# Two attentions of a decoder: issuing scores, maxima and values by whole steps of two key chunks

## The chip, the cores and the metric

The kernel runs on one core of a Trainium2 chip. The metric is device time in microseconds (us) of one launch; lower is better. Three runs of the kernel before gave 3532.81, 3535.61 and 3540.02 us, median 3535.61.

Five engines work side by side, each through its own queue of instructions: TensorE (PE; its weight loads are shown apart as PEld), VectorE (DVE), ScalarE (ACT), GpSimd (POOL) and SyncE (SP, which here only issues DMAs). They are held in order by semaphores. Matrix products land in PSUM, which has 8 banks of 128 partitions x 512 fp32 numbers.

## The reference

Four decoder layers follow one another on x (8 batches x 256 tokens x 128). Each layer adds a cross-attention over a context of 1601 tokens x 64 per batch, and then a feed-forward block. Attentions 0 and 3 are alike: 16 heads of width 8. With q, k and v projected from the layer norm of x and from the context, cut to what matters:

```python
scores = jnp.einsum('bhqd,bhkd->bhqk', qh, kh) * scale      # 256 x 1601 for each of 16 heads
attn = jax.nn.softmax(scores, axis=-1)
out = jnp.einsum('bhqk,bhkd->bhqd', attn, vh)
x = x + out.transpose(0, 2, 1, 3).reshape(B, LQ, D_MODEL) @ Wo + bo
```

Attentions 1 and 2 and the feed-forward blocks are other functions of the kernel, which the change does not touch.

## The kernel before

`narrow` computes attentions 0 and 3. Its work is cut into 32 **units**: 8 batches, and in each four groups of four heads (n = 4b + i). A unit goes through the keys in 13 chunks of 128 (the last has 65), two chunks to a **step**, so 7 steps p = 0 to 6; the last step has one chunk. The four heads of a unit lie in two tiles of K and Q, t = 0 and 1, with two heads each (g = 0 and 1), in rows 0 to 63 and 64 to 127. Each step is cut into two **half steps**, one for each t.

Three kinds of work run through each other on PE:

- **Scores**, `score(p, t, e)`, L1069: for two chunks and two heads, four matmuls of K (64 rows x 128 keys as weights) with Q (256 queries) into two banks `st`. ACT takes the exponential of each bank (L1072) into the tile `e`, which holds all four heads of one step and has two buffers. The maximum of each row is already subtracted: the shift lies in extra rows of Q.
- **Values**, `values(c, e)`, L1081: for one chunk, the four heads' `e` times V, each head in its own 32 columns of the array, summed over the 13 chunks in the one bank `ov`. Each of these fp32 products is shown as two matmuls, so a chunk is 8. The values of a step are issued in the step after it, from the list `before`. When the last chunk is done, ACT copies the bank (L1085) and SP sends it off by two DMAs (L1087, L1088).
- **Maxima**, `maxima(n)`, L873 and L876: before a unit starts, the largest score of each of its rows is needed. For this all scores are computed a first time with queries as weights: 14 pieces for a unit, each a `pair` of matmuls in two banks `pm` (g = 0 and 1; 64 rows x 128 queries, 512 keys wide). DVE reduces each bank with a TENSOR_REDUCE. Pieces 7 and 14 are narrow (66 keys, both halves of the queries in one bank, four matmuls). Then `shift` (three small DVE instructions) and, later, `place_shift` (a transpose on PE, L895, a copy on ACT and two DMAs) put the result into Q.

PSUM is divided by `psum(m=3, s=4, o=1)`: three banks `m` for the maxima, four banks `s` for the scores and for all side work (`bank()`), one `o` for the values. The banks of each kind are handed out in turn, and an instruction that writes a bank waits until the last reader of the bank's former use is done.

The order of instructions is written by hand (`manual_schedule`): the order in which the functions call is the order in each engine's queue. `plan(m)` gives the 14 pieces of the maxima of unit m to slots, one slot for each half step: from slot DONE of unit m - 2 to slot DONE of unit m - 1, with the shift in the last of them. DONE is 8 of 14. So in most half steps there is one piece, of the unit after the next or of the next. In the first unit, all 14 pieces of unit 1 stand in its first DONE slots.

`beside` is a list of side work with the share of the unit at which each piece is due: placing K and Q of unit n + 3 by DMA (L846 on SP; L855 and L856 on POOL), `place_shift`, and, by the head group i of the unit, the next batch's turned input and queries (i = 0: L808, L814), its K (i = 0: L777), its V (i = 1: L834), the end of the batch before (i = 2: two reciprocals on DVE, L907, and the projection, L913), and the turned context of the batch after the next (i = 2, attention 0: L761; attention 3 loads it ready). From unit 26 on (AFTER), pieces of the next block's first batch join it.

A half step issues, in this order: the four scores of its t; one chunk of values of the step before, if one is left; the side work that is due; the maxima of its slot.

Of the kernel before, what the change touches and what calls it, by code (L numbers as in the profile page):

```python
# [49 lines left out]
TAKEN = -3.0e38  # L50
KW = LK + 1
RING = 4
DONE = 8
AFTER = 26


# [1 line left out]
def decoder_kernel(ctx: ExitStack, tc: tile.TileContext, a: dict, out: bass.AP):  # L58
# [36 lines left out]
    def load_later(n):  # L95
        for out, in_ in later[:n]:
            nc.sync.dma_start(out=out, in_=in_)
        del later[:n]
# [248 lines left out]
    def run(steps, names):  # L347
        for name in names:
            for step in steps:
                if name in step:  # L350
                    step[name]()
# [322 lines left out]
    def narrow(wq, wkT, wvT, wo, bq, bk, bv, bo, first, after=None, last=None):  # L674
# [8 lines left out]
        with ExitStack() as es:  # L683
# [174 lines left out]
            def place(n, t):  # L858
                place_keys(n, t)
                place_queries(n, t)  # L860

            def maxima(n):

                mx = two.tile([P, QT, 4, 4], F32, tag="mx", name="mx", bufs=3)
                last = KW - 1536

                def pair(t, js, at, w):
                    k, q = K[n % RING][t], Q[n % RING][t]
                    pt = [pm() for g in range(2)]
                    for x, j in enumerate(js):  # L870
                        for g in range(2):
                            r = slice(64 * g, 64 * g + 64)
                            nc.tensor.matmul(pt[g][:, x * w:(x + 1) * w], lhsT=q[r, j * P:(j + 1) * P],  # L873
                                             rhs=k[r, at:at + w], start=True, stop=True)
                    for g in range(2):
                        nc.vector.tensor_reduce(mx[:, js[0]:js[-1] + 1, 2 * t + g, at // 512],  # L876
                                                pt[g][:, 0:len(js) * w].rearrange("p (j k) -> p j k", k=w),
                                                AX.X, ALU.max)

                def shift():  # L880
                    m = two.tile([P, QT, 4], F32, tag="mxn", name="mxn")
                    nc.vector.tensor_reduce(m, mx, AX.X, ALU.max, negate=True)
                    mq = M[n % 2].rearrange("p j (h s) -> p j h s", s=8)
                    nc.vector.tensor_copy(mq[:, :, :, 0], m)
                    nc.vector.tensor_tensor(mq[:, :, :, 1], m, mq[:, :, :, 0].bitcast(F32), ALU.subtract)

                order = [(j, at) for at in (0, 512, 1024) for j in range(QT)]
                return [f for t in range(2) for f in
                        (*(lambda j=j, t=t, at=at: pair(t, (j,), at, 512) for j, at in order),
                         lambda t=t: pair(t, range(QT), 1536, last))], shift  # L890
# [116 lines left out]
            before = []  # L1007
            steps = (NC + 1) // 2
            per = 2 * steps
            tasks = {}  # L1010

            def plan(m):

                pairs, shift = maxima(m)
                first_, last_ = max(0, per * (m - 2) + DONE), per * (m - 1) + DONE
                for x, f in enumerate(pairs):
                    tasks.setdefault(first_ + (last_ - first_) * x // len(pairs), []).append(f)
                tasks[last_ - 1].append(shift)

            plan(1)  # L1020
            for n in range(units):
                b, i = divmod(n, 4)
                v = V[b % 2]
                if n + 2 < units:
                    plan(n + 2)

                beside = []
                if n + 3 < units:
                    beside += [((0.0, 0.25)[t], lambda t=t: place(n + 3, t)) for t in range(2)]
                beside.append((0.3, lambda: load_later(3)))  # L1030
                if n + 1 < units:
                    beside.append(((DONE + 1) / per, lambda: place_shift(n + 1)))
                if b + 1 < NB and i == 0:
                    beside += zip((0.0, 0.2, 0.5, 0.65, 0.8, 1.0),
                                  (lambda: turn_y(b + 1), lambda: make_q(b + 1), *make_k(b + 1)))
                if b + 1 < NB and i == 1:
                    beside += zip((0.2, 0.4, 0.6, 0.8), make_v(b + 1))
                if b and i == 2:
                    beside += zip((0.2, 0.35, 0.6), finish(b - 1))
                if b + 2 < NB and i == 2:  # L1040
                    load_ct(b + 2)
                    if first:
                        cuts, turns = make_ct(b + 2)
                        beside += zip((0.0, 0.0, 0.4, 0.6), cuts)
                        beside += zip((0.3, 0.5, 0.7, 0.9), turns)
                if b + 3 < NB and i == 3:
                    beside.append((0.0, lambda: load_raw(b + 3)))
                if b + 2 < NB and i == 3:
                    beside.append((0.5, lambda: (make_y(b + 2), add_bias(b + 2))))
                if after is not None and n >= AFTER:  # L1050
                    if n == AFTER:
                        late = after(left(), bank)
                    beside += [((x - per * (n - AFTER)) / per, lambda x=x: run([late[x]], EARLY + LATE))
                               for x in late if x // per == n - AFTER]
                beside.sort(key=lambda x: x[0])
                if i == 0:
                    od[b] = two.tile([P, LQ], F32, tag="od", name="od")
                    sums[b] = two.tile([P, LQ], F32, tag="sums", name="sums")
                cell = {}

                def score(p, t, e):
                    k, q = K[n % RING][t], Q[n % RING][t]
                    cs = range(2 * p, min(2 * p + 2, NC))
                    m = P if cs[-1] < NC - 1 else LAST
                    st = [bank().rearrange("p (j q) -> p j q", q=LQ) for g in range(2)]
                    for j, c in enumerate(cs):
                        for g in range(2):
                            r = slice(64 * g, 64 * g + 64)
                            nc.tensor.matmul(st[g][0:m, j, :], lhsT=k[r, c * P:c * P + m], rhs=q[r, :],  # L1069
                                             start=True, stop=True)  # L1070
                    for g in range(2):
                        nc.scalar.activation(e[0:m, 2 * t + g, 0:len(cs), :], st[g][0:m, 0:len(cs), :], AF.Exp)  # L1072

                def values(c, e, cell=cell, i=i, v=v, b=b):
                    if c == 0:
                        cell["o"] = ps["o"].tile([P, LQ], F32, tag="o", name="ov")
                    m = P if c < NC - 1 else LAST
                    for g in range(4):
                        h = 4 * i + g
                        at = 2 * D * c + 32 * (h // 2) + 2 * (h % 2)  # L1080
                        nc.tensor.matmul(cell["o"][32 * g:32 * g + 32, :], lhsT=v[0:m, at:at + 32],  # L1081
                                         rhs=e[0:m, g, c % 2, :], start=(c == 0), stop=(c == NC - 1))
                    if c == NC - 1:
                        os = two.tile([P, LQ], F32, tag="os", name="os")
                        nc.scalar.copy(os, cell["o"])  # L1085
                        at = slice(32 * i, 32 * i + 32)
                        nc.sync.dma_start(out=od[b][at, :], in_=os[0:P:4, :])  # L1087
                        nc.sync.dma_start(out=sums[b][at, :], in_=os[1:P:4, :])  # L1088

                for p in range(steps):  # L1090
                    e = two.tile([P, 4, 2, LQ], F32, tag="e", name="e")
                    for t in range(2):
                        score(p, t, e)
                        if n == p == 0:
                            spare(6)
                        if before:
                            before.pop(0)()
                        while beside and (beside[0][0] * 2 * steps < 2 * p + t + 1 or p * t == steps - 1):
                            beside.pop(0)[1]()
                        for f in tasks.pop(per * n + 2 * p + t, []):  # L1100
                            f()
                    before = [lambda c=c, e=e, values=values: values(c, e)
                              for c in range(2 * p, min(2 * p + 2, NC))]
            *inverses, project = finish(NB - 1)
# [829 lines left out]
```

## Time and profile before

The table is of one profiled execution. Its span, from the first instruction to the last, is 3529.4 us; the median of the runs is 3535.61 us, 6.2 us more.

| stage | from - to, us | PE busy | DVE busy | ACT busy | POOL busy | PE clock |
|---|---|---|---|---|---|---|
| attention 0 (units) | 55.5 - 706 | 643.1 | 535.6 | 519.9 | 297.3 | 0.99 |
| the blocks between | 706 - 2686 | 1873.4 | 1354.3 | 1200.1 | 607.2 | 0.98 |
| attention 3 (units) | 2686 - 3317 | 625.5 | 536.6 | 500.9 | 212.4 | 1.00 |
| the last block | 3317 - 3529.4 | 202.3 | 121.2 | 57.3 | 21.6 | 1.00 |

| unit by head group, steady | attention 0, us | attention 3, us |
|---|---|---|
| i = 0 | 20.82 | 20.82 |
| i = 1 | 21.10 | 21.10 |
| i = 2 | 20.28 | 19.19 |
| i = 3 | 17.83 | 17.77 |

How to read it: a unit's length is the time from its first score to the next unit's first score. PE's busy time is a union of matmul times whose ends are modelled, so a PE that is busy all the time can still have stretches in which nothing new begins; the starts of matmuls and of weight loads (PEld) tell more. In a row of the timeline stand start, length, engine, line, operation, out<-in, count, and in brackets the idle time of that engine before the row with what ended it. In a row of a stage stand its stretch and length, then the busy time and the number of instructions of each engine, the PE clock, the DMA share and GB/s.

### The profile page before, as it was taken

The numbers are of one execution on the slowest core, as the hardware profiler recorded it, in microseconds if no ns is written. First come the engines' busy times: TensorE is split into PE (matmuls) and PEld (weight loads), VectorE is DVE, ScalarE is ACT, GpSimd is POOL, SyncE is SP. The second block draws the span as 40 slices with busy tenths as digits, with TensorE's granted clock in tenths as the row PEclk, the third lists the DMA queues.
The fourth block names the chain that finished last, engine by engine and source line by source line (L and its number), as shares of the span: only waits on it lengthen the run. The fifth ranks groups of instructions, "written<-read, shape, count | busy, mean of one in ns | idle before, by whom it ended". The sixth has DMA issues, their size and how long they took to land.

```text
span 3529.4 us, 75160 instructions
## 1 busy us (share of the span) xinstructions
PE 3380.6 (96%) x28453; PEld 2299.7 (65%) x28453; DVE 2580.6 (73%) x6482; ACT 2290.0 (65%) x5747; POOL 1179.4 (33%) x2105
## 2 busy tenths in 40 slices
PE   7999999989999999999999999988999999999999
PEld 4555555468787877788787878866445555555444
DVE  6888888656776767676776767675557888888665
ACT  3888887746666666667666666654224878787622
POOL 6344344624152513324151520131115333332100
PEclk8999999989999999999999999999998999999999
DMA  5544444120001001000100000021004444443100
GB/s 97 89 73 74 71 77 58 19 83 1 15 1 33 2 1 39 1 15 1 39 1 22 6 1 15 1 66 33 1 0 85 78 63 68 65 69 53 41 5 7
DMA packets 113449, 130.24 MB, mean 37 GB/s; under 512 B 67616, under 2 KB 96832, under 8 KB 112448
## 3 DMA queue, kind: packets, MB, share of 16 engines
q1 hardware_dynamic: 92352, 114.22, 18.0%
q0 software_dynamic: 20480, 10.53, 1.3%
q8 instruction: 225, 3.69, 0.4%
q10 hardware_dynamic: 256, 0.69, 0.1%
q14 instruction: 136, 1.11, 0.1%
HBM read 44.79 MB, written 11.28 MB: 16 GB/s over the span
## 4 chain that ended last, share of the span: by engine, by line
PE 81%; DVE 9%; ACT 6%; POOL 2%; issue 2%; DMA 0%; DVEq 0%; POOLq 0%; SPq 0%; ACTq 0%
PE ov L1081 13%; PE o L514 12%; PE st L467 12%; PE pm L873 11%; PE t L500 8%; PE st L1069 6%; PE gu L1740 3%; PE o L1789 3%; PE gu L1741 3%; ACT pt L502 3%; DVE ls L474 2%; DVE mx L876 2%; ACT e L488 2%; PE st L834 1%; DVE ql L444 1%
## 5 line engine op out<-in xcount | busy, mean ns | idle before, releaser
L876 DVE TENSOR_REDUCE mx<-pm 128x1 f32<-128x512 f32 (+1 forms) x1792 | 1020.3, 627 | 172.7 <-PE pm L873 168.9
L1072 ACT ACTIVATE e<-st 128x512 f32<-128x512 f32 (+1 forms) x1792 | 910.6, 566 | 210.5 <-PE st L1069 160.0
L474 DVE TENSOR_REDUCE ls<-st 128x1 f32<-128x512 f32 x1088 | 549.5, 567 | 292.3 <-PE st L467 291.2
L488 ACT ACTIVATE e<-st,ls 128x512 f32<-128x512 f32 x1088 | 634.0, 602 | 13.4 <-DVE ls L477 12.6
L502 ACT COPY pt<-t 128x512 f32<-128x512 f32 x544 | 293.6, 586 | 460.8 <-PE t L500 459.9
L1081 PE MATMUL ov<-e,V 128*32 128x256 f32 x6656 | 564.6, 392 | 0.3 <-ACT e L1072 0.3
L873 PE MATMUL pm<-K,Q 64*128 64x512 f32 (+1 forms) x2048 | 497.3, 451 | 18.6 <-DVE mx L876 15.4
L500 PE MATMUL t<-ident,e 128*128 128x128 f32 (+1 forms) x3536 | 506.5, 281 | 2.6
L514 PE MATMUL o<-pt,v 128*64 128x128 f32 (+1 forms) x7072 | 490.2, 278 | 17.0 <-DVE pt L502 13.0
L514 PEld LDWEIGHTS o<-pt,v 128*64 128x64 f32 (+1 forms) x7072 | 412.1, 137 | 88.2 <-DVE pt L502 37.2
L873 PEld LDWEIGHTS pm<-K,Q 64*128 64x128 f32 x2048 | 226.1, 187 | 325.8 <-DVE mx L876 223.3
L500 PEld LDWEIGHTS t<-ident,e 128*128 128x128 f32 (+1 forms) x3536 | 391.5, 141 | 52.4 <-ACT pt L502 30.0
L467 PE MATMUL st<-ct,qh 128*128 128x512 f32 x1088 | 406.1, 373 | 1.8 <-ACT e L488 1.8
L1069 PE MATMUL st<-Q,K 64*128 64x256 f32 (+1 forms) x3328 | 403.1, 287 | 0.1
L467 PE MATMUL st<-ct,ql 128*128 128x512 f32 x1088 | 362.9, 367 | 0.0
L1069 PEld LDWEIGHTS st<-Q,K 64*128 64x128 f32 (+1 forms) x3328 | 333.1, 182 | 32.3 <-issue 6.5
L855 POOL DMA_DIRECT2D Q<-qh x256 | 128.3, 501 | 450.5 <-PE st L1069 422.9
L502 DVE COPY pt<-t 128x512 f32<-128x512 f32 (+1 forms) x544 | 239.1, 481 | 34.9 <-PE t L500 34.8
L467 PEld LDWEIGHTS st<-ct,qh 128*128 128x128 f32 x1088 | 205.6, 189 | 86.3 <-issue 34.9
L1081 PEld LDWEIGHTS ov<-e,V 128*32 128x32 f32 x6656 | 142.5, 108 | 153.7 <-issue 37.9
L1742 ACT ACTIVATE act<-gu 128x512 f32<-128x512 f32 x130 | 77.5, 597 | 243.2 <-PE gu L1741 232.1
L488 ACT ACTIVATION_READ_ACCUMULATOR e<-st,ls 128x1 f32 x1088 | 230.7, 212 | 0.0
(545 smaller groups left out, 4302.2 us busy)
## 6 DMA issues: line engine op xcount, KB each, us to landing
K<-kh SPq DMA_DIRECT2D x250, 100.1 KB
K<-kl SPq DMA_DIRECT2D x250, 100.1 KB
ct<-ctd SPq DMA_DIRECT2D x23, 801.0 KB
ctd<-ct SPq DMA_DIRECT2D x8, 801.0 KB
v<-in_ctx SPq DMA_DIRECT2D x16, 384.0 KB
Q<-qh POOLq DMA_DIRECT2D x256, 16.0 KB, 2.7
Q<-ql POOLq DMA_DIRECT2D x256, 16.0 KB, 3.0
raw<-in_ctx SPq DMA_DIRECT2D x8, 384.0 KB
```

The source lines that it names most:

```text
L467: nc.tensor.matmul(st[n, c][:, 0:w], lhsT=q[k, h][i][:, j * P:(j + 1) * P], rhs=ct[k][:, at:at + w], start=(i == 0), stop=(i == 1))
L474: nc.vector.tensor_reduce(ls[n][:, c:c + 1], st[n, c][:, 0:BANK[c][1]], AX.X, ALU.max)
L488: nc.scalar.activation(e[n][:, at:at + w], st[n, c][:, 0:w], AF.Exp, bias=ls[n][:, 4:5], scale=1.0, accum_out=ls[n][:, 5 + c:6 + c])
L500: nc.tensor.transpose(t[0:m, (c - 4 * i) * P:(c - 4 * i + 1) * P], e[n][:, c * P:c * P + m], ident)
L502: (nc.scalar.copy if i < 2 else nc.vector.tensor_copy)(p[0:m, 0:w], t[0:m, 0:w])
L514: nc.tensor.matmul(o[n][half, 0:P], lhsT=v[k][0:m, c, :], rhs=turned[n, c // 4][0:m, (c % 4) * P:(c % 4 + 1) * P], start=(c < 2), stop=(c ...
L855: nc.gpsimd.dma_start(out=q[r:P:8, :].bitcast(F32), in_=qhl[b][r % 2][src, :].bitcast(F32))
L873: nc.tensor.matmul(pt[g][:, x * w:(x + 1) * w], lhsT=q[r, j * P:(j + 1) * P], rhs=k[r, at:at + w], start=True, stop=True)
L876: nc.vector.tensor_reduce(mx[:, js[0]:js[-1] + 1, 2 * t + g, at // 512], pt[g][:, 0:len(js) * w].rearrange("p (j k) -> p j k", k=w), AX.X, ...
L1069: nc.tensor.matmul(st[g][0:m, j, :], lhsT=k[r, c * P:c * P + m], rhs=q[r, :], start=True, stop=True)
L1072: nc.scalar.activation(e[0:m, 2 * t + g, 0:len(cs), :], st[g][0:m, 0:len(cs), :], AF.Exp)
L1081: nc.tensor.matmul(cell["o"][32 * g:32 * g + 32, :], lhsT=v[0:m, at:at + 32], rhs=e[0:m, g, c % 2, :], start=(c == 0), stop=(c == NC - 1))
```

## The change

The two half steps of a step become one whole step. It issues the maxima of the step's first slot; the scores of both t, eight matmuls into all four banks `st`; the maxima of the second slot; the side work that is due in the step; and then all values of the step before, two chunks (16 matmuls) one behind the other. DONE goes from 8 to 6, so the maxima of a unit, its shift and `place_shift` stand one step earlier. The numbers of banks, the matmuls, the reductions and the exponentials stay as they are; `psum(m=3, s=4, o=1)` is unchanged.

```diff
-DONE = 8
+DONE = 6
...
                 for p in range(steps):
                     e = two.tile([P, 4, 2, LQ], F32, tag="e", name="e")
+                    first_, last_ = (tasks.pop(per * n + 2 * p + t, []) for t in range(2))
+                    for f in first_:
+                        f()
                     for t in range(2):
                         score(p, t, e)
                         if n == p == 0:
                             spare(6)
-                        if before:
-                            before.pop(0)()
-                        while beside and (beside[0][0] * 2 * steps < 2 * p + t + 1 or p * t == steps - 1):
-                            beside.pop(0)[1]()
-                        for f in tasks.pop(per * n + 2 * p + t, []):
-                            f()
+                    for f in last_:
+                        f()
+                    while beside and (beside[0][0] * 2 * steps < 2 * p + 2 or p == steps - 1):
+                        beside.pop(0)[1]()
+                    for f in before:
+                        f()
                     before = [lambda c=c, e=e, values=values: values(c, e)
                               for c in range(2 * p, min(2 * p + 2, NC))]
```

## The prediction

> **What bounds the kernel now.** I read the page's busy times and groups first, then busy time by stage, then the timeline of single steps. The two stages that the change touches, attention 0 (55 to 706 us) and attention 3 (2686 to 3317 us), fill 1281 us of a span of 3529.4 us; the rest is not touched. The page:
>
> ```profile
> PE 3380.6 (96%) x28453; PEld 2299.7 (65%) x28453; DVE 2580.6 (73%) x6482; ACT 2290.0 (65%) x5747; POOL 1179.4 (33%) x2105
> ...
> L876 DVE TENSOR_REDUCE mx<-pm 128x1 f32<-128x512 f32 (+1 forms) x1792 | 1020.3, 627 | 172.7 <-PE pm L873 168.9
> L1072 ACT ACTIVATE e<-st 128x512 f32<-128x512 f32 (+1 forms) x1792 | 910.6, 566 | 210.5 <-PE st L1069 160.0
> ...
> L873 PEld LDWEIGHTS pm<-K,Q 64*128 64x128 f32 x2048 | 226.1, 187 | 325.8 <-DVE mx L876 223.3
> ```
>
> The weight loads of the maxima (L873) have 325.8 us idle before them, 223.3 of it put down to the reductions of L876. The four units of one batch in attention 0, by busy time in each (PE, PEld, DVE, ACT, POOL), in the order of head groups 3 (of the batch before), 0, 1 and 2:
>
> ```profile
> 270.87:288.70 17.83, 17.83 (x181) 10.16 (x183) 15.63 (x30) 14.82 (x32) 8.62 (x19) 1.00 0.49 106
> 288.70:309.50 20.80, 20.80 (x222) 11.03 (x220) 18.26 (x34) 16.91 (x36) 5.71 (x11) 1.00 0.63 95
> 309.50:330.60 21.10, 21.10 (x214) 11.51 (x206) 17.02 (x33) 17.59 (x36) 13.01 (x23) 1.00 0.38 57
> 330.60:350.90 20.30, 20.30 (x213) 11.76 (x210) 17.33 (x33) 16.21 (x35) 6.40 (x13) 1.00 0.33 47
> ```
>
> PE is never idle in the record, DVE comes next, and the clock is full. A unit without side work takes 17.8 us; side work (projections of the next batch) brings the others to 20 or 21. One quiet half step, as the timeline of PE shows it (start, length):
>
> ```profile
> 309.76 0.50 PE L873 MATMUL pm<-K,Q 64*128 64x512 f32 x2
> 310.09 0.40 PE L1069 MATMUL st<-Q,K 64*128 64x256 f32 x4
> 310.42 0.64 PE L1081 MATMUL ov<-e,V 128*32 128x256 f32 x8
> 310.99 0.54 PE L873 MATMUL pm<-K,Q 64*128 64x512 f32 x2
> 311.32 0.44 PE L1069 MATMUL st<-Q,K 64*128 64x256 f32 x4
> 311.70 0.64 PE L1081 MATMUL ov<-e,V 128*32 128x256 f32 x8
> 312.27 0.50 PE L873 MATMUL pm<-K,Q 64*128 64x512 f32 x2
> ```
>
> Starts give the costs: maxima 0.33, scores 0.33, values 0.57, in all 1.23, and 1.28 for the second half step, where a load waited 0.05 for DVE. A whole step is 2.51 us. Inside these: 0.11 of the maxima is their exposed weight load (the next load starts 0.11 after it), 0.22 the stream; the scores stream 0.22 and stand 0.11 before the values; the second four values start at 310.66, 0.24 after the first, so two waves are 0.48 and 0.09 is left before the next load.
>
> **Part 1, fewer changes of tile shape: a gain.** Per step the values come once, 16 matmuls at 0.57 + 2 x 0.24 = 1.05 instead of 2 x 0.57 = 1.14; one exposed maxima load (0.11) and one stand before the values (0.11) go. PE's own work of a quiet step would be 0.33 + 2 x 0.22 (scores) + 0.22 (second pair) + 0.11 + 1.05 = 2.15 instead of 2.46: 0.31 a step, if nothing waits.
>
> The row shows 0.41 us of idle weight loading after every group of values, whatever follows. The Trainium skill's TensorEngine Tiling (Array Packing), Key Properties, says that a change of tiling mode drains the array; by that rule alone the change gains in every step, about 0.3 x 448 steps = 140 us.
>
> **Part 2, the fourth bank that isn't there: a new wait.** A pair of maxima takes two banks of three. The step now issues pair A, eight scores, pair B, values. A holds banks x and y, B needs z and then x again. So B's second matmul waits until DVE has reduced A's first. Before, the values stood between any two pairs and covered this. The trace has the same sequence at the start of attention 0, where two pairs are due in one slot (weight loads):
>
> ```profile
> 63.01 0.29 PEld L873 LDWEIGHTS pm<-K,Q 64*128 64x128 f32 x3 [0.33 <-DVE mx L876]
> 64.29 0.18 PEld L873 LDWEIGHTS pm<-K,Q 64*128 64x128 f32 x1 [0.99 <-DVE mx L876]
> 64.29 0.52 PEld L1069 LDWEIGHTS st<-Q,K 64*128 64x128 f32 x4
> 64.95 0.16 PEld L1081 LDWEIGHTS ov<-e,V 128*32 128x32 f32 x8
> ```
>
> The fourth load stands 0.99 us and comes 1.28 us after the first; the scores behind it, which need nothing of it, start at the same 64.29. The parts: a reduction starts 0.53 after its pair's first load (63.01 to 63.55), takes 0.69, and the release 0.05. The eight scores now placed in between hide up to 0.33 + 0.44 = 0.77 of it, so some 0.5 stays, and the load behind the wait is exposed again (0.11). In the queue behind it stand the side work, 16 values and the next pair A; all wait.
>
> The row at 64.29 shows PE passing nothing ahead of the waiting load. The Trainium skill's TensorE: Matmul & The Clock Gate, Part 3 (what overlaps and what doesn't), has matmuls in strict program order, only weight loads being pulled ahead; by it the values cannot fill the wait either.
>
> A quiet step is then 1.28 + 0.11 + 0.22 + 0.10 (stand) + 1.05 = **2.75 us against 2.51**. DVE (reductions every 0.608 us when fed: 2.43 a step) is no longer the limit there, and ACT is not either: in the single records its exponentials follow 0.49 us apart, 1.97 a step.
>
> **A unit after, step by step.** p=0 has 8 values (the odd last chunk): 1.28 + 0.43 + 0.57 = 2.28, but DVE's 2.43 holds. p=1, 3, 4, 5: 2.75. p=2 (DONE is 6 now, so B is the narrow pair, 66 keys): the wait is the same, the stream 0.17: 2.60. p=6 (A narrow): a narrow reduction starts 0.45 after its load and takes 0.30 (304.16, 304.61), so B's second load comes at 0.80 and the step is 0.80 + 0.43 + 1.05 = 2.28. Sum 2.43 + 4 x 2.75 + 2.60 + 2.28 = 18.31, with place_shift 0.32 (2965.46 to 2965.78) **18.63 against 17.8**: +0.8. This already counts what the change wins at a unit's start, where the first values now wait 0.65 us for the exponentials (the half steps there take 1.22, 0.65 and 1.90) and later come a step after them.
>
> Side work costs the same as before, as it is placed between pair B and the values, one stand more and one less: a K part 0.66 (313.50 to 314.16), a V part 1.04 (2958.41 to 2959.45). Group 0 has 3.45 of it and goes to 18.31 + 3.45 - 0.17 (p=0 no longer held by DVE) = 21.6 from 20.8; group 1 has 3.71 and goes to 22.0 from 21.1; group 2, whose two reciprocals (942 ns each) delay the reductions in both kernels, I take at the others' +0.8. ACT's copies of side work now stand behind four exponentials, not two; in a step with a K part the copy ends 0.77 + 1.97 + 0.69 = 3.43 us after the step's start, and the scores that want its bank come at 3.41 + 0.55 = 3.96, so this is hidden; if not, it costs up to 0.6 for each of about 13 copies a batch.
>
> **Other moves, at nothing.** At a unit's start the K and Q placements are issued on SP and POOL before the copy of the last values and its two DMAs; what they fetch is used 8 steps later, and the sums three units later. place_shift comes one step earlier, with 3 steps (8 us) for a DMA of about 2. The single values bank is emptied behind p=0's exponentials at about 3.2 us after the unit's start; it is wanted at about 4.1. If that 0.9 were gone, it would cost that per unit at most.
>
> **The ends.** Units 30 and 31 have few pairs left and much side work: there part 1 alone counts, 0.3 x some 10 steps x 2 attentions = -6 us. The first unit has two pairs more in it (DONE), which the last ones lack: nothing, within 2 us. Between them 58 units x 0.8 = 46. **Sum +40 us** on the profiled execution, span 3529.4 to 3569. Its span lies 6.2 us under the median of the runs (3535.61), which holds launch and ends, so the forecast is **3576 us**.
>
> Bounds of what the trace doesn't show: sixteen values in one run may take 0.57 + 2 x 0.21 (nearest below: the pure stream) or 2 x 0.57 (each chunk as now): 0.99 to 1.14, or -0.3 to +0.5 a unit; I keep 1.05, by the 0.24 between waves. Group 2 may gain its wait back in the reciprocals' shadow: 0 to +1.2. Together +0.2 to +1.3 a unit: +6 to +70 us.
>
> **The rivals.**
> - Faster (0.09). B's second load comes earlier than 1.05 us after A's first (2.51 less 0.11 + 0.22 + 0.10 + 1.05 = 1.03): that is the point at which the step breaks even. Then DVE is the bound, 16.4 us for a bare unit, 18.3 in group 2, PE 18.5 in groups 0 and 1: about -1.9 a unit, 3536 - 110 = 3426 at best. For it: the 0.41 gaps are real. Against: 1.28 in the row above, with nothing in it that scores could shorten.
> - No change (0.06). Values at 0.99 and group 2 gaining: +0.1 a unit, 3541 and below.
> - Worse (0.12). The wait also delays ACT's releases: side work behind four exponentials holds the scores' banks, +0.6 on the 13 copies x 8 x 2, 3576 + 60 to 70 = 3640. For it: four banks are all used by one step now. Against: the 3.43 and 3.96 above.
> - It doesn't do what it says (0.01): the order of PE's instructions of the changed kernel shows pair, eight scores, pair, side work, values. Excluded but for that.
> - The forecast's own band has 0.72: 3550 to 3610.
>
> The chances of faster by over 0.2%, within it (about what a measurement of this kernel can tell from no change) and slower are 0.09, 0.06, 0.85. The range takes the forecast's band and its bounds on both sides, with parts of the no-change and worse cases: 3541 to 3610.
>
> **What would show it.** In the changed profile: half of L873's loads idle before B's second with DVE mx named, the fourth load 1.28 after the first; quiet steps 2.75 apart; PE record no longer gapless; values in runs of 16 that last 1.05 between starts; idle time of L876 up. It is wrong if a quiet step is under 2.5, if the fourth load comes under 1.05, or if units with side work stretch by more than 1.3.

## The result, and the profile after

Four runs of the changed kernel gave 3591.26 to 3602.63 us, median 3596.52; the kernel before, in four runs beside and ahead of them, had a median of 3537.82. The ratio is 1.0167 with a 95% interval of 1.0146 to 1.0189: **slower by 52 to 67 us**, where 40 had been forecast.

The page after, busy times and the groups that were shown of before:

```profile
PE 3389.4 (94%) x28453; PEld 2341.4 (65%) x28453; DVE 2570.4 (71%) x6482; ACT 2244.9 (62%) x5747; POOL 1179.8 (33%) x2105
...
L876 DVE TENSOR_REDUCE mx<-pm 128x1 f32<-128x512 f32 (+1 forms) x1792 | 1012.1, 627 | 242.1 <-PE pm L873 236.3
L1072 ACT ACTIVATE e<-st 128x512 f32<-128x512 f32 (+1 forms) x1792 | 869.6, 571 | 350.0 <-PE st L1069 347.6
...
L873 PEld LDWEIGHTS pm<-K,Q 64*128 64x128 f32 x2048 | 278.1, 191 | 381.2 <-DVE mx L876 306.2
```

The same instructions, as many, and each about as long (627 ns for a reduction in both, 566 and 571 for an exponential); what grew is idle time. The maxima's weight loads stand 306.2 us for DVE (223.3 before), and at the same time the reductions stand 236.3 us for those very matmuls (168.9 before): two engines that wait for each other in turn, neither full. ACT has 347.6 us of waiting for scores (160.0 before). One quiet step, weight loads of PE:

```profile
315.41 0.19 PEld L873 LDWEIGHTS pm<-K,Q 64*128 64x128 f32 x2 [0.41 <-DVE mx L876]
315.52 0.66 PEld L1069 LDWEIGHTS st<-Q,K 64*128 64x128 f32 x8
316.11 0.18 PEld L873 LDWEIGHTS pm<-K,Q 64*128 64x128 f32 x1
316.69 0.18 PEld L873 LDWEIGHTS pm<-K,Q 64*128 64x128 f32 x1 [0.40 <-DVE mx L876]
317.12 0.59 PEld L1081 LDWEIGHTS ov<-e,V 128*32 128x32 f32 x16 [0.24 <-issue]
318.12 0.18 PEld L873 LDWEIGHTS pm<-K,Q 64*128 64x128 f32 x2 [0.41 <-DVE mx L876]
```

The first pair is loaded at 315.41, the second pair's first matmul at 316.11, its second at 316.69: 1.28 us after the first, 0.40 of it spelled out as a wait for DVE. The 16 values behind it start at 317.12 and last 1.00. The step takes 2.71 us; before it took 2.51.

Where the profiled execution's 65.6 us lie (3529.4 to 3595.0; a unit runs from its first score to the next one's, unit 31 to its last score):

| stretch | before, us | after, us | difference |
|---|---|---|---|
| up to the first score | 55.5 | 59.3 | +3.8 |
| first units of the two attentions | 28.92 + 29.00 | 37.66 + 36.44 | +16.2 |
| units 1 to 29 | 583.3 + 566.4 | 604.3 + 585.3 | +39.9 |
| units 30 and 31 | 38.0 + 35.7 | 37.0 + 36.1 | -0.6 |
| between the attentions, and the end | 2192.6 | 2198.9 | +6.3 |

The first row, and the stretch ahead of attention 3 in the last, hold a part of the change: the three pairs of maxima in the first slot now stand ahead of the first score. Weight loads at the start of attention 0:

```profile
56.70 0.30 PEld L873 LDWEIGHTS pm<-K,Q 64*128 64x128 f32 x3
...
59.18 0.18 PEld L873 LDWEIGHTS pm<-K,Q 64*128 64x128 f32 x1 [0.42 <-DVE mx L876]
```

The first score's load comes at 59.25, 2.55 us behind the first of these; in attention 3 the same takes 2.77 us (2720.95 to 2723.72). What else the two rows hold, 1.3 and 3.5 us, no run takes apart. The timed difference, 58.7 us, is 6.9 smaller than the profiled one. Wherever a run's span and time are both on record, the time is 1.7 to 1.8 us more than the span; by that the profiled execution of the kernel before took about 3531.1 us, 6.7 less than its median, while that of the changed kernel took its median. By head group a steady unit went from 20.82 to 21.52, 21.10 to 21.75, 20.28 to 21.34 (attention 3: 19.19 to 19.93) and 17.83 to 18.38.

### The profile page after: what moved, and what is told of

The parts are those of the page before. It is cut to its first block, busy times and chain, and to the rows that moved or that the text cites. A ratio compares the mean times of both kernels' runs of the same rounds, so it can differ in the third digit from the quotient of the medians.

```text
span 3595.0 us, 75249 instructions
## 1 busy us (share of the span) xinstructions
PE 3389.4 (94%) x28453; PEld 2341.4 (65%) x28453; DVE 2570.4 (71%) x6482; ACT 2244.9 (62%) x5747; POOL 1179.8 (33%) x2105
## 4 chain that ended last, share of the span: by engine, by line
PE 71%; DVE 18%; ACT 7%; issue 2%; POOL 2%; DMA 1%; SPq 0%; POOLq 0%; DVEq 0%; ACTq 0%
PE o L514 12%; PE st L467 11%; PE ov L1081 10%; DVE mx L876 10%; PE pm L873 10%; PE t L500 8%; PE o L1792 3%; PE gu L1744 3%; PE gu L1743 3%; ACT pt L502 3%; DVE ls L474 2%; ACT e L488 2%; PE st L834 1%; DVE ql L444 1%; PE st L777 1%
## 5 line engine op out<-in xcount | busy, mean ns | idle before, releaser
L876 DVE TENSOR_REDUCE mx<-pm 128x1 f32<-128x512 f32 (+1 forms) x1792 | 1012.1, 627 | 242.1 <-PE pm L873 236.3
L1072 ACT ACTIVATE e<-st 128x512 f32<-128x512 f32 (+1 forms) x1792 | 869.6, 571 | 350.0 <-PE st L1069 347.6
L873 PE MATMUL pm<-K,Q 64*128 64x512 f32 (+1 forms) x2048 | 607.2, 440 | 66.3 <-DVE mx L876 40.2
L873 PEld LDWEIGHTS pm<-K,Q 64*128 64x128 f32 x2048 | 278.1, 191 | 381.2 <-DVE mx L876 306.2
L1081 PE MATMUL ov<-e,V 128*32 128x256 f32 x6656 | 459.4, 391 | 0.5 <-ACT os L1085 0.5
L1069 PE MATMUL st<-Q,K 64*128 64x256 f32 (+1 forms) x3328 | 296.9, 286 | 2.3 <-ACT e L1072 1.5
L1069 PEld LDWEIGHTS st<-Q,K 64*128 64x128 f32 (+1 forms) x3328 | 263.6, 184 | 29.7 <-ACT e L1072 11.8
L1081 PEld LDWEIGHTS ov<-e,V 128*32 128x32 f32 x6656 | 172.4, 110 | 158.8 <-issue 75.2
L467 PEld LDWEIGHTS st<-ct,ql 128*128 128x128 f32 x1088 | 206.1, 189 | 37.1
```

Source lines behind the costliest of these rows:

```text
L467: nc.tensor.matmul(st[n, c][:, 0:w], lhsT=q[k, h][i][:, j * P:(j + 1) * P], rhs=ct[k][:, at:at + w], start=(i == 0), stop=(i == 1))
```

## The experiments

Ratios are to runs of the kernel before taken beside each. Times are medians; unit lengths and stretches are from one profiled execution of each kernel.

**Is it the reduction's length? e1 and e2** read half as many columns in each wide reduction, in the new order and in the old.

```diff
-  pt[g][:, 0:len(js) * w].rearrange("p (j k) -> p j k", k=w),
+  pt[g][:, 0:len(js) * w].rearrange("p (j k) -> p j k", k=w)[:, :, 0:256 if w == 512 else w],
```

> The changed kernel, with DVE reducing only the first 256 of the 512 columns of each wide bank of maxima (it leaves half of the keys out of the row maximum; PE, ACT and the waits stay). Theory (the second pair's second matmul waits for the first pair's first reduction): that reduction ends about 0.26 us earlier (0.68 us for 512 columns and 0.29 for 132 give 1.03 ns a column), so the fourth load comes 1.02 us after the first instead of 1.28, a quiet step takes 2.45 instead of 2.71, and 5 to 6 steps of each of some 60 units win 0.26: -80 to -95 us, 3500 to 3515. Rival (the long run of values, ACT's banks or the side work's new place take the time): DVE's length does not matter, 3590 to 3597.

> The control: the same halved reductions in the kernel before. Theory: there only every second half step waits for DVE, by 0.05 us, and the reciprocals of group 2 are covered better: 5 x 0.05 x 60 = -15 us, up to -25 with group 2: 3513 to 3523. If it wins as much as e1 (-80), a long reduction hurts both orders alike and e1 says nothing on the new order.

Measured: e1 3497.95 us, e2 3501.57 us, beside 3539.29 for the kernel before (ratios 0.9880, 0.9852 to 0.9908; 0.9889, 0.9861 to 0.9917). The new order won 99 us, the old 38; the two are now level. In the profiles the new order won 97 us: 70 in units 1 to 29 of the two attentions and 21 in their first units, which take 26.8 and 26.7 us. Both times are below their ranges, by 2 and 11 us. A quiet step of e1, weight loads:

```profile
365.46 0.18 PEld L873 LDWEIGHTS pm<-K,Q 64*128 64x128 f32 x2 [0.41 <-issue]
365.57 0.65 PEld L1070 LDWEIGHTS st<-Q,K 64*128 64x128 f32 x8
366.15 0.50 PEld L873 LDWEIGHTS pm<-K,Q 64*128 64x128 f32 x2
366.90 0.59 PEld L1082 LDWEIGHTS ov<-e,V 128*32 128x32 f32 x16 [0.25 <-issue]
367.90 0.18 PEld L873 LDWEIGHTS pm<-K,Q 64*128 64x128 f32 x2 [0.41 <-DVE mx L876]
```

The second pair is now one row, of 0.50: its second load ends at 366.65 and, at 0.18 long, began about 366.47, 1.01 us after the first. The step is 2.44. That is the theory to 0.01 us. The control won more than its expectation (38 against 15 to 25): the old order was held by DVE more widely than by 0.05 a step, most of all in group 2 (20.28 to 20.01 and 19.19 to 18.20) and at units without side work (17.8 to 17.5).

**Is it the missing bank? e9 to e12** vary the number of banks and the order, two by two. The score loop runs over `range(2 - t)` heads and the values read `e[.., min(g, 2), ..]`; e10 and e12 add:

```diff
-            es.enter_context(psum(m=3, s=4, o=1))
+            es.enter_context(psum(m=4, s=3, o=1))
```

> First of four that give the maxima a fourth bank. To free one, the fourth head of each unit gets no scores and no exponentials (its values read the third head's); everything else is as in the changed kernel. A step then needs three banks of scores. This one keeps three banks of maxima and four of scores: the base. Both theories: units as in the changed kernel or up to 0.1 shorter (18.3 without side work), quiet step 2.71, 3580 to 3597.

> As the one before, with four banks of maxima and three of scores. Theory (the missing fourth bank makes the wait): no load of a second pair waits for the first pair's reduction, PE needs 2.1 us a step and DVE's 2.43 to 2.5 hold; a unit without side work falls from 18.4 to 16.6 to 17.2; steps with side work win little, as that now stands for one of three score banks: 3525 to 3560. Rival (the wait comes from the order itself, from a drain or from ACT): within 5 us of the three-bank run.

> The kernel before with the same head left out, three banks of maxima and four of scores: units as before or up to 0.3 shorter, as the first values of a unit wait less for ACT (17.5 to 17.8 without side work): 3515 to 3537.

> The kernel before with the same head left out, four banks of maxima and three of scores. Theory: the order of half steps never stood on that bank for more than 0.05 us in a step: within 10 us of the three-bank run below, or a little above where side work now waits for a score bank; and with the bank there the whole steps win: e10's units without side work are 0.4 to 0.9 shorter than these. Rival (whole steps lose whatever the banks): e10's units stay longer than these.

| | whole steps | half steps |
|---|---|---|
| 3 banks of maxima: all, us | 3612.60 | 3516.68 |
| units by head group, attention 3 | 21.39, 21.76, 19.94, 18.39 | 20.35, 20.46, 19.14, 17.27 |
| 4 banks of maxima: all, us | 3481.30 | 3476.36 |
| units by head group, attention 3 | 19.91, 19.98, 18.26, 16.49 | 19.96, 20.28, 18.15, 16.94 |

With the bank, the whole steps win 131 us and the half steps 40. A part of that is the granted clock (e9's runs 0.969 to 0.975, e10's 0.977 to 0.984); in units 1 to 29 of attention 3, where it was 1.00 in all four profiles, the whole steps go from 586.0 to 534.0 us and the half steps from 553.9 to 540.0. The scores lose a bank at the same time; a step here needs three. The units of the new order are, with the bank, shorter by 0.45 us where there is no side work, as expected of the bank theory; over the whole kernel the two orders come out level. (The new order's first units are longer there, 29.7 and 29.8 us against 26.0 and 29.0, at clocks of 0.89 and 0.89 against 1.00 and 0.88, which takes back most of the 7 us of its units 1 to 27.) Three expectations were off in size. e10 came out below its range, since units with side work won 1.5 to 1.8 us too. e12 was to be within 10 us of e11 and won 40: as in e2, the old order stands for DVE's bank more than the 0.05 us of a quiet step tells. e9 spread from 3598.85 to 3619.70 and lay above its range; its steps are those of the changed kernel (2.71). Weight loads and DVE of e10:

```profile
363.80 0.19 PEld L873 LDWEIGHTS pm<-K,Q 64*128 64x128 f32 x2 [0.41 <-DVE mx L876]
363.90 0.53 PEld L1069 LDWEIGHTS st<-Q,K 64*128 64x128 f32 x5
364.28 0.18 PEld L873 LDWEIGHTS pm<-K,Q 64*128 64x128 f32 x1
364.37 0.18 PEld L1069 LDWEIGHTS st<-Q,K 64*128 64x128 f32 x1
364.49 0.18 PEld L873 LDWEIGHTS pm<-K,Q 64*128 64x128 f32 x1
364.92 0.59 PEld L1081 LDWEIGHTS ov<-e,V 128*32 128x32 f32 x16 [0.24 <-issue]
365.92 0.19 PEld L873 LDWEIGHTS pm<-K,Q 64*128 64x128 f32 x2 [0.41 <-DVE mx L876]
```

```profile
361.76 9.04 DVE L876 TENSOR_REDUCE mx<-pm 128x1 f32<-128x512 f32 x16
```

The second pair follows the scores at once (364.28, 364.49), the step takes 2.12 us, and DVE runs 16 reductions with no gap over 0.1 us. PE's own 2.15 us of the prediction is seen only here (with six scores in the step, which alone change nothing: e9's quiet step is 2.71 too). It is what the fewer changes of shape bring in a step where neither the bank nor DVE holds PE; over a whole unit without side work e10 is 0.45 us shorter than e12.

The repeated 0.40 before each second pair of the changed kernel is what the Trainium skill's Perfetto Trace Analysis, Optimization Strategy, calls consistent bubbles, a possible sign that PSUM has no room for the next tile; here e10, in whose quiet steps they are gone, confirms that reading.

**Can the wait be filled? e5 and e6** put the side work between the scores and the second pair; e6 does so only in steps that have such work on PE, keeps half steps elsewhere and in the first unit, and plans the maxima one half step later (DONE = 9, pairs ahead of the scores, which is the order of before).

```diff
-                    for f in last_:
-                        f()
                     while beside and (beside[0][0] * 2 * steps < 2 * p + 2 or p == steps - 1):
                         beside.pop(0)[1]()
+                    for f in last_:
+                        f()
```

> The changed kernel with the side work of a step moved from behind the second pair of maxima to ahead of it, between the scores and that pair. Theory (PE stands some 0.5 us for the first reduction before the second pair): a projection of 0.66 us fills the stand, at the price of one more change of tile shape, so a step with such work goes from 3.37 to about 3.0 and one with place_shift alone from 3.03 to 2.75: groups 0 to 3 at 19.6, 20.0, 20.2 and 18.1, some -5 us a batch, 3515 to 3535. Rival (the time lies in the run of 16 values or in ACT's copies behind four exponentials): the place makes no difference or, with one more change of shape in each, +0.1 for each of 14 pieces a batch: 3596 to 3620.

> Whole steps, with the side work between the scores and the second pair, only where a step has side work on PE; half steps, as in the kernel before, in all others and in the first unit; the maxima of the first unit as before (20 pieces). Theory: steps without side work stay at 2.51, steps with a K part go from 3.16 (before) to about 2.95: -0.2 in each of some 14 steps a batch, 3480 to 3505 against 3538. Rival (the whole step loses wherever it stands): 3545 or more.

Measured: e5 3663.66 us (ratio 1.0351, 1.0327 to 1.0376), e6 3620.12 (1.0230, 1.0215 to 1.0245), e5 above even its rival's range, e6 on its rival's side. Weight loads of e5, a step with a K part:

```profile
346.80 0.19 PEld L873 LDWEIGHTS pm<-K,Q 64*128 64x128 f32 x2 [0.41 <-DVE mx L876]
346.90 0.66 PEld L1069 LDWEIGHTS st<-Q,K 64*128 64x128 f32 x8
348.28 0.19 PEld L777 LDWEIGHTS st<-ct,wkh 128*128 128x128 f32 x1 [0.71 <-ACT e L1072]
348.39 0.19 PEld L777 LDWEIGHTS st<-ct,wkl 128*128 128x128 f32 x1
348.94 0.18 PEld L873 LDWEIGHTS pm<-K,Q 64*128 64x128 f32 x2 [0.37 <-DVE mx L876]
349.37 0.59 PEld L1081 LDWEIGHTS ov<-e,V 128*32 128x32 f32 x16 [0.24 <-issue]
350.37 0.19 PEld L873 LDWEIGHTS pm<-K,Q 64*128 64x128 f32 x2 [0.41 <-DVE mx L876]
```

The K part does not start behind the scores, but at 348.28, 1.48 us after the step's start, and the row names ACT: its bank `st` is the one of the step's own first scores, as all four are taken, and comes free only when the first exponential is done. Behind the wait for DVE's bank, which ends 1.28 us into the step, lay a second one for ACT's, which ends at 1.48; with the side work ahead the second pair comes after both, and one change of shape more. My expectation had left this bank out. In e6 the steps with side work are as long as in e5 or longer, while its other steps (2.51) and its first units (26.5 us) are as before or shorter: it loses in the whole steps alone. So a filler that needs a score bank did not help: in these steps PSUM is short on both sides, and what is missing is not work to put in the gap.

**e7: does the same wait show in the old order?** The lone last chunk's values move to the second half step of the next unit.

```diff
-                        if before:
+                        if len(before) > (p == t == 0):
                             before.pop(0)()
```

> The kernel before with the lone last chunk's values moved from the first to the second half step of a unit, so that the first values of the new unit, which now wait 0.65 us for the exponentials, come later. Theory: the first three half steps (3.77 us) shrink by 0.2 to 0.3, where DVE allows it: -5 to -20 us, 3518 to 3533. If nothing: those exponentials or the copy of the last values hold it again, 3536 to 3540.

Measured: 3551.61 us, ratio 1.0043 (1.0027 to 1.0059): a miss. The step p=1 fell from 3.13 to 2.64 us as meant, but p=0 rose from 1.87 to 2.50. Weight loads there:

```profile
326.61 0.29 PEld L873 LDWEIGHTS pm<-K,Q 64*128 64x128 f32 x3 [0.63 <-DVE mx L876]
...
327.27 0.16 PEld L1081 LDWEIGHTS ov<-e,V 65*32 65x32 f32 x8
...
328.67 0.16 PEld L1081 LDWEIGHTS ov<-e,V 128*32 128x32 f32 x8 [0.30 <-ACT os L1085]
```

Two pairs now have only scores between them, and the load stands 0.63 us for a reduction: the new wait of the change, made in the old order by taking eight values away. The next values then stand 0.30 for the copy that empties their single bank.

**What does DONE cost? e3** is the changed kernel with DONE = 8, **e4** the kernel before with DONE = 6; one line each.

> The changed kernel with DONE back at 8, so only the whole-step order is left of the change. Theory: the first unit of each attention has 20 pieces of maxima in it and not 22, and 14 of them in four steps and not three: its 37.7 and 36.4 us shrink by 3 to 6 each; in the other units the narrow pieces move to the first pair of p=0 and the second of p=3, worth about -0.1 a unit: 3575 to 3588. Rival (the first unit's 8 us more come from the whole-step order itself, with the clock falling to half in it): first units unchanged, 3588 to 3597.

> The kernel before with DONE at 6 and nothing else. Theory: the first units carry two pieces more (2 x 1.25 us each) and the last ones two fewer; in the steady units the narrow piece leaves the place where it let two pairs follow each other in 0.65 us, so that the pairs of p=0 wait, while the first values of p=1 wait for ACT anyway: 3537 to 3548. Rival (DONE is what costs most of the 59 us): above 3560.

Measured: e3 3589.19 us (ratio 1.0136, 1.0101 to 1.0171), e4 3554.55 (1.0040, 1.0024 to 1.0055), above its range by 7. e3's first units shrank by 3.4 and 6.8 us, to 34.3 and 29.6, as its theory had it, but the units of group 0 grew by 0.3 (21.84), so that the sum stayed just above the range, at the lower edge of the rival's, whose condition (unchanged first units) did not hold. In e4 the steady units of groups 0, 1 and 3 are as before (20.80, 20.99, 17.71) and those of group 2 are 0.5 us longer (20.77 and 19.65), but its first units are 39.2 and 36.8 us long. The first units of the two attentions, the whole stretch of each; behind the stretch, its length and the busy times of PE, PEld, DVE, ACT and POOL stands PE's clock, third from the end. Before (attention 0), after, e4, e3:

```profile
55.46:84.38 28.92, 26.14 (x219) 13.97 (x220) 22.78 (x41) 18.36 (x36) 12.23 (x19) 1.00 0.44 84
```

```profile
59.28:96.94 37.66, 35.03 (x221) 19.89 (x223) 23.49 (x44) 16.88 (x35) 9.84 (x16) 0.68 0.27 48
2723.72:2760.16 36.44, 34.25 (x221) 19.76 (x223) 23.65 (x44) 16.29 (x35) 9.81 (x16) 0.67 0.18 32
```

```profile
55.43:94.66 39.23, 35.95 (x225) 18.82 (x226) 24.32 (x45) 18.47 (x36) 12.06 (x19) 0.70 0.31 62
2702.06:2738.81 36.75, 32.85 (x226) 17.28 (x226) 24.35 (x45) 17.67 (x36) 11.64 (x19) 0.80 0.25 51
```

```profile
58.01:92.32 34.31, 31.81 (x219) 17.25 (x221) 22.78 (x42) 16.70 (x35) 10.94 (x18) 0.80 0.33 59
2722.95:2752.57 29.62, 26.64 (x219) 14.80 (x221) 22.77 (x42) 16.20 (x35) 9.85 (x16) 1.00 0.26 56
```

With DONE at 6 (after and e4), DVE does 0.7 to 1.6 us more work than before; the units take 7 to 10 more. Fourteen pieces in six slots instead of eight put two and three pairs behind each other instead of one and two, each second one waits as above, and the granted clock was at half for 23.9 us of each first unit of the changed kernel. The clock also differs where the order does not: e3's two first units have the same order of instructions and take 34.3 us at 0.80 and 29.6 at 1.00.

**e8: is it the clock?** Six matmuls that nobody reads stand behind each group of maxima in the first four steps of an attention's first unit.

```diff
                     for f in first_:
                         f()
+                    if n == 0 and p < 4:
+                        warm(6)
...
+            def warm(n):
+                pt = bank()
+                for _ in range(n):
+                    nc.tensor.matmul(pt[:, 0:LQ], lhsT=wkh, rhs=K[0][0][:, 0:LQ], start=True, stop=True)
```

> The changed kernel with six idle matmuls (their results are read by nobody) behind each group of maxima in the first four steps of an attention's first unit, some 48 matmuls of 0.11 us. Theory (the first unit's 37.7 and 36.4 us come from waits for reductions that let the granted clock fall to 0.5 for 24 us): the clock stays up more of the time and the first units take 30 to 34 in spite of the added work: -4 to -14 us, 3582 to 3592. Rival (the waits alone make the length, the clock is only their sign): first units as long or longer by up to 5: 3596 to 3606.

Measured: 3608.45 us, ratio 1.0200 (1.0184 to 1.0215): on the rival's side, 2 us above its range.

```profile
59.62:96.51 36.89, 33.11 (x263) 20.61 (x264) 22.30 (x42) 16.88 (x35) 9.72 (x15) 0.95 0.26 42
2727.26:2771.83 44.57, 41.58 (x263) 26.55 (x264) 21.96 (x42) 16.38 (x35) 9.79 (x16) 0.70 0.12 18
```

In attention 0 the clock stayed at 0.95, and the unit took 36.9 us with 48 matmuls more, 0.14 us apart (6.7 us in all); in attention 3 it fell all the same, and the first 24 of them stood 0.25 apart. If the added matmuls cost their full time in the first, the clock accounts for about 7 of the 8.7 us there; if they filled waits, for less. This run does not tell the two apart.

The other profiles tell more. No first unit in any run that kept its clock at 0.99 or above is longer than 29.7 us; all that are longer had less. A low clock does not need DONE = 6: in e11, the half steps with DONE = 8 and one head fewer, the first units of the profiled execution (the slowest of seven) took 36.7 us at 0.67 and 32.8 at 0.84, where e12, with a bank more, has 26.0 at 1.00 and 28.9 at 0.88. So the clock is a large part of the 7 to 10 us. That DONE = 6 alone costs time is shown by e4's ten runs (15 us by the medians). How much of that is waits, and how much a clock that falls more, stays open: no kernel with DONE = 6 and whole reductions kept the full clock in its first units.

No version that does the whole computation beat the kernel before. e1 and e2 point to what would: shorter reductions, worth 38 us in the old order. They take the row's shift from half of the keys, which leaves the softmax the same as long as no exponential overflows, and gives up the guarantee that none does.

## Why the prediction was right, and where it was off

- **The new wait: right, and its size.** Forecast 1.28 us from the first load to the fourth, measured 1.28; e1 shortens it by the reduction's 0.27, e10 removes it.
- **Quiet step: 2.75 forecast, 2.71 measured.** The mis-sized term is the run of 16 values, put at 1.05 and measured at 1.00: the first two waves are 0.24 apart and the others 0.215, near the lower bound of the text. The step p=0, put at DVE's 2.43, took 2.27 where it has no side work, which is PE's own sum (2.28). Hence the units: 21.6, 22.0 and 18.63 forecast for groups 0, 1 and 3, 21.5, 21.75 and 18.38 measured.
- **Group 2: +0.8 forecast, +1.06 in attention 0 and +0.74 in attention 3.** The order of size is right, but e2 shows that DVE held this group more than I had counted, and in e4 DONE alone lengthens it by 0.5.
- **Fewer changes of shape: right in the working, invisible in the result.** 2.15 us of PE's own work a step is 2.12 in e10. In the changed kernel the 0.3 is there, and the wait takes it back with 0.2 more. The drain that the Trainium skill's TensorEngine Tiling (Array Packing), Key Properties, states is in keeping with e10's shorter step. A gain of 140 us, as by that rule alone, is shown by no run here: with the bank there, units 1 to 27 of both attentions gain 7 us in all (e10 against e12).
- **Side work at the same cost: right, with a cover that the text did not name.** A step with a K part takes 3.37, the quiet 2.71 and 0.66. The text looked at the bank only after the copy; e5 shows that the side work's own bank comes free no sooner than 1.48 us into the step. Where the change puts it, behind the second pair, PE gets there at 1.70 (323.05 to 324.75 in the timeline after), so the second pair's wait is what hides it.
- **The first unit: wrong.** "Nothing, within 2 us" for the two added pairs was +8.7 and +7.4 us, and 2.55 and 2.77 more ahead of the first scores: together a third of the profiled loss. The step that failed treated the pieces as a count of reductions; that they stand closer, with the new wait between them, that the first slot's now come ahead of the first score, and that the clock is lower there (0.68 and 0.67 instead of 1.00) was left out. e4, with DONE alone, has first units as long.
- **The ends: -6 forecast, -0.6 measured** for units 30 and 31. Unit 31, with no maxima left, won 0.7 and 1.3 us; unit 30 won 0.3 in attention 0 and lost 1.7 in attention 3, for which no run was made.
- **Two smaller sums of the text do not hold.** The 6.2 us between span and median were put down to launch and ends. Those take 1.7 to 1.8; the rest is that the profiled execution was quicker than the median. And the price of the worse rival, 0.6 us on 13 x 8 x 2 copies, is 125 us, not 60 to 70. The step with a K part shows none of it: its 3.37 us are the quiet step and the side work's own 0.66.

Together: units 1 to 29 +40 instead of +46, the first units with what stands ahead of them +21 instead of 0, the last two -1 instead of -6. The sum fell short by about 20 us, nearly all of it the first units', as the other two misses cancel. The stated range still held the result, but it had been worked out from the steady units, with nothing in it for the first ones; so far that is luck.

## What to carry to other kernels

When instructions are grouped to save changes of an engine's shape, first count the buffers that the group holds at once: a pair that needs a bank which its neighbour still holds waits for that neighbour's reader, and in a strict queue everything behind it waits too. Spacing such pairs evenly was what had hidden the reader; the trace of before showed the price at a place where two pairs already followed each other (1.28 us from the first load to the fourth). And before filling a gap with other work, ask which bank that work writes.

## What the runs showed of the hardware that I had not expected

The granted clock was at 0.5 in the first units of both attentions of the changed kernel (59.3 to 76.4 and 79.8 to 86.7 us; 2725.2 to 2749.1), although the longest stretch there without a matmul on record is 0.7 us. Before, it stayed at 1.0 in the same units, with stretches of up to 0.56. It is not one execution's alone: the mean clock over the whole span was 0.973 to 0.982 in the four runs of the changed kernel and 0.981 to 0.988 in 31 of the kernel before.

What makes it fall stays open. It is tempting to name the many short stands. But the first falls come 0.1 and 1.4 us after the first score of their units, so what lies ahead has a part in them; and in the first unit of attention 3 in e12 no stretch without a matmul is longer than 0.11 us, PE is busy for 28.3 of its 28.9 us, and the clock (third from the end) was at 0.5 all the same:

```profile
2677.20:2684.00 6.80, 6.80 (x41) 3.04 (x41) 5.39 (x11) 2.87 (x5) 1.89 (x2) 0.50 0.01 1
```

The Trainium skill's TensorE: Matmul & The Clock Gate, Part 1, has the clock fall after an idle window of about 3.4 us. No stretch that long without a matmul is on record ahead of these falls: in the 24 us ahead of the first, the longest is 3.0 us, and it ended 8.7 us earlier.
